# A fused RWKV and mixture-of-experts layer: the first block in halves, two of the last rows ahead of a branch, and three row accumulations between scatters

## The chip, the cores and the metric

One core of a Trainium2 chip. The metric is the device time of one execution in microseconds (us). Five engines take part, each with an instruction stream of its own: PE (TensorE, matrix products and transposes), DVE (VectorE), ACT (ScalarE), POOL (GpSimd) and SP (SyncE, which here only issues DMAs). POOL issues DMAs too: the gathers, and all DMAs that accumulate into DRAM.

## What is computed

The input x is 2048 rows of 512. Everything is float32. Cut to what matters:

```python
xn  = layernorm(x)
rvk = xn @ W_rvk.T;  r, v, k = split(rvk, 3)
att = (sigmoid(r) * wkv(time_decay, time_first, k, v)) @ W_out.T    # wkv: a recurrence over all rows
# experts: 8 routed and 4 that hand on their input, the 2 best of 12 for each row
probs = softmax(xn @ classifier_w.T); idx = top_k(probs + bias, 2); rw = 1.5 * probs[idx]
ffn = sum over the chosen e < 8: rw_e * (silu(xn @ gate_e.T) * (xn @ up_e.T)) @ down_e.T
ffn = ffn + xn * (sum of rw over the chosen e >= 8)
out = x + att + ffn
```

## The kernel before, in words

The rows stand in 16 row tiles of 128 (numbered 0 to 15), four to a block (blocks 0 to 3). The order of the instructions on every engine is the order in which the code issues them (a manual schedule); nothing reorders them later. A wait arises where a tile's producer, or the last user of its buffer, runs on another engine or is a DMA.

*Head.* SP issues the four loads of block 0 (L95), the weights of k (L102), the classifier, and the other loads. `norm(b)` (L207) takes mean and variance of four row tiles on DVE (L212, L213), then one short chain for all four: an ACT square root (L218), a reciprocal and a Newton step on DVE (L220 to L227). Then the four tiles are normalized, the even ones on DVE (L232), the odd ones on ACT (L234), and stored to DRAM as `xs` for the later gathers (L125). `turn_block(b)` (L237) transposes the block on PE, 4 chunks of 4 tiles, and ACT copies each chunk out of PSUM (L246). Blocks 1 to 3 follow in a loop, with first products (L325) and the classifier (L254, L267) between. Then comes the routing on DVE, which sorts the 4096 choices into tiles of 128 rows of one expert each.

*Middle.* The work of the scans (DVE, 16 of them: 4 blocks by 4 chunks), of the k, v, r products, and of 25 expert tiles is merged by planned times (`table`, L991 to L1025). An expert tile i is gathered from `xs` (L733, POOL), transposed by a DMA, multiplied by gate and up weights (L795, PE), activated (L803 ACT, L804 and L806 DVE), transposed again, multiplied by the down weights (L836, PE), scaled on ACT into `yo` (L840, three buffers in turn) and scattered with an add into the output (L841, POOL). The output has been set to x beforehand. Tiles are about 10.3 us apart.

The output projection of rows 0 to 7 (`attention_row`, L969) is merged in as well: PE products (L973), then DVE adds the share of the experts that hand on their input (L983). Rows 0 to 3 are accumulated into the output by POOL DMAs in two pairs (`add_row`, L967); rows 4 to 7 are put on the list `late`.

*Tail.* Behind the table, `attention(NTB - 2, [j])` does rows 8 to 11 (PE L921, DVE L934), between them the last scan's steps. Then comes a branch (L1032 to L1053): the number of tiles that are needed is loaded into every engine, and a loop over further tiles is skipped when there are no more than 25. Behind the branch `read_out` reads rows 12 to 15 of the output back (L900, SP) and adds the experts that hand on their input (L901, DVE). POOL accumulates rows 4 to 11 (L1057, L967). `attention(NTB - 1)` multiplies rows 12 to 15 (L921), adds the result on DVE (L930) and stores the row (L931); row 15 goes in two halves of 256 columns, both in one PSUM bank.

All writes into the output tensor are ordered: a scatter or an accumulation that may touch the same rows as an earlier one waits on POOL until the earlier one's data has landed. Row accumulations of different rows do not wait for each other.

PSUM has eight banks in four pools of two: `ps_mm`, `ps_gu`, `ps_o` and `ps_tr`. Row 8 to 11 take `ps_o` and `ps_mm` in turn; rows 12 and 13 take `ps_o`, 14 and 15 `ps_mm`.

Of the kernel before, what the change touches and what calls it, by code (L numbers as in the profile page):

```python
# [26 lines left out]
F32 = mybir.dt.float32  # L27
# [8 lines left out]
P = 128  # L36
T = 2048
C = 512
CC = C // P
TB = 512  # L40
NTB = T // TB
NJ = TB // P
# [9 lines left out]
TILES = 25  # L52
# [7 lines left out]
def layer(ctx: ExitStack, tc: tile.TileContext, x, w_rvk, w_out, decay, first, cls, ebias, gu, down, out):  # L60
    nc = tc.nc

    def pool(name, bufs, **kw):
        return ctx.enter_context(tc.tile_pool(name=name, bufs=bufs, **kw))
# [3 lines left out]
    place = pool("place", 1)  # L68
# [6 lines left out]
    small = pool("small", 2)  # L75
# [4 lines left out]
    ps_mm = pool("ps_mm", 2, space=bass.MemoryType.PSUM)  # L80
    ps_gu = pool("ps_gu", 2, space=bass.MemoryType.PSUM)
    ps_o = pool("ps_o", 2, space=bass.MemoryType.PSUM)
    ps_tr = pool("ps_tr", 2, space=bass.MemoryType.PSUM)
# [38 lines left out]
    def store_xn(b):  # L122
        for j in range(NJ):
            i = b * NJ + j
            nc.sync.dma_start(xs[i * P : (i + 1) * P, :], xt[i])  # L125
# [65 lines left out]
    for c in range(CC):  # L191

        s = const.tile([P, 5], F32, tag=f"state{c}", name=f"state{c}")
# [10 lines left out]
    xnT = {}  # L204
    pl = ps_o.tile([P, NT, ET], F32, tag="o", name="pl")

    def norm(b):  # L207
        js = slice(b * NJ, (b + 1) * NJ)
        for j in range(NJ):
            i = b * NJ + j  # L210
            st = small.tile([P, 6], F32, tag="st", name=f"st{i}")
            nc.vector.bn_stats(st, xt[i])  # L212
            nc.vector.bn_aggr(mv[:, i, :], st)  # L213
        var = mv[:, js, 1]
        ve = small.tile([P, NJ], F32, tag="ve", name=f"ve{b}")
        nc.vector.tensor_scalar_add(ve, var, EPS)
        sd = small.tile([P, NJ], F32, tag="sd", name=f"sd{b}")
        nc.scalar.activation(sd, var, AF.Sqrt, bias=eps_sb[:, 0:1])  # L218
        r0 = small.tile([P, NJ], F32, tag="r0", name=f"r0{b}")
        nc.vector.reciprocal(r0, sd)  # L220

        sq = small.tile([P, NJ], F32, tag="sq", name=f"sq{b}")
        nc.vector.tensor_mul(sq, r0, r0)
        nc.vector.tensor_mul(sq, sq, ve)
        nc.vector.tensor_scalar(sq, sq, -0.5, 1.5, ALU.mult, ALU.add)
        nc.vector.tensor_mul(rstd[:, js], r0, sq)
        nc.vector.scalar_tensor_tensor(shift[:, js], mv[:, js, 0], -1.0, rstd[:, js], ALU.mult, ALU.mult)  # L227
        for j in range(NJ):
            i = b * NJ + j
            t, r = xt[i], rstd[:, i : i + 1]  # L230
            if j % 2 == 0:
                nc.vector.tensor_scalar(t, t, mv[:, i, 0:1], r, ALU.subtract, ALU.mult)  # L232
            else:
                nc.scalar.activation(t, t, AF.Identity, bias=shift[:, i : i + 1], scale=r)  # L234
        store_xn(b)

    def turn_block(b):  # L237
        xnT[b] = place.tile([P, CC, TB], F32, tag=f"s{2 + b}", name=f"xnT{b}")
        for c in range(CC):
            if c % 2 == 0:  # L240
                pt = ps_tr.tile([P, TB], F32, tag="tr", name=f"pt{b}_{c}")
            else:
                pt = ps_gu.tile([P, TB], F32, tag="gu", name=f"pt{b}_{c}")
            for j in range(NJ):
                nc.tensor.transpose(pt[:, j * P : (j + 1) * P], xt[b * NJ + j][:, c * P : (c + 1) * P], ident)
            nc.scalar.copy(xnT[b][:, c, :], pt)  # L246

    lgs = {}

# [261 lines left out]
    def whole(gen):  # L511
        for _ in gen:
            pass


    manual = ExitStack()
    manual.enter_context(tc.manual_schedule())
    norm(0)
    turn_block(0)
    for b in range(NTB):  # L520
        if b + 1 < NTB:
            norm(b + 1)
        fill(1 if b else 2)
        logits(b)
        fill(1 if b else 3)
        if b + 1 < NTB:
            turn_block(b + 1)
        add_quarters(b)
# [194 lines left out]
    wplace = const.tile([P, MAX_TILES], F32, tag="wplace", name="wplace")  # L723
# [109 lines left out]
    def finish(i, weight=wplace, to=to_i):  # L833
        po = ps_o.tile([P, C], F32, tag="o", name=f"po{i}")
        for c in range(IC):
            nc.tensor.matmul(  # L836
                po, st[i]["actT"][:, c, :], st[i]["d"][:, c, :], start=(c == 0), stop=(c == IC - 1)
            )
        yo = rows.tile([P, C], F32, tag="rb", name=f"yo{i}")
        nc.scalar.activation(yo, po, AF.Identity, scale=weight[:, i : i + 1])  # L840
        nc.gpsimd.indirect_dma_start(  # L841
            out=out,
            out_offset=bass.IndirectOffsetOnAxis(ap=to[:, i : i + 1], axis=0),
            in_=yo,
            in_offset=None,
            compute_op=ALU.add,
        )
        del st[i]

    def first_half(i, n):  # L850
# [15 lines left out]
    def second_half(i, n):  # L866

        if i + 1 < n:
            unite(i + 1)
        if i + 2 < n:  # L870
            flip(i + 2)
        if i > 1:
            finish(i - 2)
        if 1 < i < n - 1:
            fetch_down(i)
        if i == n - 2:
            fetch_down(i + 1)
        if i == n - 1:
            finish(i - 1)

    xrows, orows = {}, {}
# [12 lines left out]
    def read_out(b):  # L894

        t = place.tile([P, NJ, C], F32, tag="s0", name=f"orows{b}")
        for j in range(NJ):
# [4 lines left out]
                orows[i], xrows[i], zw[:, i : i + 1], orows[i], ALU.mult, ALU.add  # L902
            )

    def attention(b, js=range(NJ)):

        for j in js:
            i = b * NJ + j
            if b < NTB - 2:
                po = ps_tr.tile([P, C], F32, tag="tr", name=f"pw{i}")  # L910
            elif j >= 2 if i in orows else j % 2 == 1:
                po = ps_mm.tile([P, C], F32, tag="mm", name=f"pw{i}")
            else:
                po = ps_o.tile([P, C], F32, tag="o", name=f"pw{i}")

            halves = 2 if i == NT - 1 else 1
            n = C // halves
            for h in range(halves):
                hs = slice(h * n, (h + 1) * n)
                for c in range(CC):  # L920
                    nc.tensor.matmul(  # L921
                        po[:, hs],
                        yT[b][:, j, c, :],
                        wout_sb[:, c, hs],
                        start=(c == 0),
                        stop=(c == CC - 1),
                    )
                    yield
                if i in orows:
                    nc.vector.tensor_add(orows[i][:, hs], orows[i][:, hs], po[:, hs])  # L930
                    nc.sync.dma_start(out[i * P : (i + 1) * P, hs], orows[i][:, hs])  # L931
            if i in orows:
                continue
            nc.vector.scalar_tensor_tensor(xrows[i], xrows[i], zw[:, i : i + 1], po, ALU.mult, ALU.add)  # L934

# [28 lines left out]
    late = []  # L964

    def add_row(n):
        nc.gpsimd.dma_start(out[n * P : (n + 1) * P, :], xrows[n], accum_op=ALU.add)  # L967
# [25 lines left out]
    def plan(at, what, *args):  # L993
        table.append((at, iter([(what, *args)]) if args else what))
# [19 lines left out]
    spread = (total - 12) / TILES  # L1014
# [4 lines left out]
    plan(7 + spread * TILES, read_xn, NTB - 1)  # L1019
    plan(4 + spread * TILES, turn_act, TILES - 1)  # L1020
    plan(7 + spread * TILES, finish, TILES - 1)
    for _, work in sorted(table, key=lambda entry: entry[0]):
        todo = next(work, None)
        if todo:
            todo[0](*todo[1:])  # L1025
    for j, stops in enumerate((1, 2, 0, 0)):
        whole(attention(NTB - 2, [j]))
        for _ in range(stops):
            next(stages[-1])


    count = nc.values_load(  # L1032
# [23 lines left out]
    read_out(NTB - 1)  # L1056
    for n in (*late, *range((NTB - 2) * NJ, (NTB - 1) * NJ)):  # L1057
        add_row(n)
    whole(attention(NTB - 1))
    manual.close()  # L1060


# [40 lines left out]
```

## Time and profile before

| what | us |
|---|---|
| median of three runs (379.75 to 383.75) | 380.06 |
| the profiled execution's own time | 379.29 |
| its span, from the first to the last instruction | 377.5 |
| busy: PE, DVE, ACT, POOL | 358.2, 308.9, 161.5, 91.4 |
| granted TensorE clock | 1.0 |

The profile is of one execution. A row of the timeline is: start, length, engine, line, operation, output<-inputs, and in brackets the idle time of the engine before it and what ended that idle time. "x16" means that so many instructions are merged into the row. A float32 product shows as two instructions of PE. A row of the chain of waits is: start, length, engine and line; "issue" is time in which nothing shows a wait. A row of DMA issues ends with the KB of one and the median us from issue to landing.

### The profile page before, as it was taken

How to read it: one execution, taken by the hardware profiler on the slowest of the kernel's cores; microseconds unless marked ns; L12 is line 12 of the kernel's file. 1: busy time of each engine (PE TensorE's matmuls, PEld its weight loads, DVE VectorE, ACT ScalarE, POOL GpSimd, SP SyncE). 2: the span in 40 equal slices, each digit the busy share in tenths (PEclk: the TensorE clock that was granted, in tenths of full speed). 3: DMA queues.
4: the chain of work that ended last, by engine and by line, in shares of the span. 5: the costliest groups of instructions: out<-in, count | busy, mean ns of one | idle time of the engine just before them, and what ended most of it. 6: DMA issues, size and time to landing. Idle time of an engine off the chain costs nothing.

```text
span 377.5 us, 3504 instructions
## 1 busy us (share of the span) xinstructions
PE 358.2 (95%) x970; PEld 164.9 (44%) x970; DVE 308.9 (82%) x450; ACT 161.5 (43%) x274; POOL 91.4 (24%) x118
## 2 busy tenths in 40 slices
PE   0899998999999999999999999999999999999995
PEld 0565444543444444444444444444444444444343
DVE  4879899989997997987987779597769786959951
ACT  1677311232653554554556453636354555423000
POOL 5000300210203233322232224133144321102450
PEclk9999999999999999999999999999999999999999
DMA  7998944643657898889898998999999999767497
GB/s 268 399 356 322 334 141 162 227 91 132 177 126 220 257 264 250 251 230 260 220 262 237 272 265 222 271 233 319 258 280 277 290 264 248 195 188 166 93 191 191
DMA packets 63029, 88.80 MB, mean 235 GB/s; under 512 B 42208, under 2 KB 42592, under 8 KB 59232
## 3 DMA queue, kind: packets, MB, share of 16 engines
q1 hardware_dynamic: 55472, 67.85, 61.5%
q0 software_dynamic: 7536, 20.71, 23.5%
q8 instruction: 8, 0.13, 0.1%
q14 instruction: 13, 0.11, 0.1%
HBM read 63.78 MB, written 19.40 MB: 220 GB/s over the span
## 4 chain that ended last, share of the span: by engine, by line
PE 73%; DVE 17%; DMA 5%; ACT 2%; issue 2%; SPq 0%; DVEq 0%
PE pg L795 22%; PE po L836 10%; PE pr L408 9%; PE py L325 9%; PE pw L973 7%; PE pz L325 6%; PE px L325 4%; PE pw L921 4%; DMA x<-in_x_dram 3%; DVE den L505 3%; DMA wrvk<-in_w_rvk_dram 2%; DVE tok L687 2%; DVE sums L490 1%; DVE obv L477 1%; DVE st L212 1%
## 5 line engine op out<-in xcount | busy, mean ns | idle before, releaser
L795 PE MATMUL pg<-gw,xgT 128*128 128x512 f32 x200 | 90.2, 593 | 1.5 <-ACT xgT L783 1.5
L841 POOL DMA_INDIRECT out_dram<-yo,to_i x25 | 45.7, 1826 | 165.0 <-ACT yo L840 114.5
L408 PE MATMUL pr<-xnT,wrvk 128*128 128x512 f32 x128 | 60.6, 593 | 0.0
L795 PEld LDWEIGHTS pg<-gw,xgT 128*128 128x128 f32 x200 | 37.8, 190 | 49.3 <-issue 45.7
L505 DVE RECIPROCAL den<-den 128x512 f32<-128x512 f32 x16 | 53.5, 3345 | 0.0
L836 PE MATMUL po<-dw,actT 128*128 128x512 f32 x100 | 46.9, 593 | 0.5 <-ACT actT L814 0.5
L803 ACT ACTIVATE th<-pg 128x256 f32<-128x256 f32 x25 | 9.6, 384 | 85.0 <-PE pg L795 85.0
L733 POOL DMA_INDIRECT xg<-xs,token_i x25 | 27.0, 1080 | 61.9 <-ACT xp L775 28.3
L408 PEld LDWEIGHTS pr<-xnT,wrvk 128*128 128x128 f32 x128 | 24.1, 190 | 29.2 <-issue 29.2
L804 DVE SCALAR_TENSOR_TENSOR th<-th,pg 128x256 f32<-128x256 f32 x25 | 10.5, 419 | 32.1 <-ACT th L803 32.0
L325 PE MATMUL px<-xnT,wrvk 128*128 128x512 f32 x64 | 32.3, 604 | 0.0
L325 PE MATMUL py<-t,wrvk 128*128 128x512 f32 x64 | 30.7, 594 | 0.0
L783 ACT COPY xgT<-xq 128x1024 uint16<-128x1024 uint16 x25 | 28.9, 1156 | 3.9 <-DMA xq<-xp 3.8
L921 PE MATMUL pw<-wout_sb,yT 128*128 128x512 f32 (+1 forms) x72 | 28.2, 548 | 2.0 <-DVE xrows L934 1.5
L973 PE MATMUL pw<-wout_sb,yT 128*128 128x512 f32 x64 | 30.1, 592 | 0.0
L836 PEld LDWEIGHTS po<-dw,actT 128*128 128x128 f32 x100 | 18.9, 190 | 24.2 <-issue 22.7
L775 ACT COPY xp<-xg 128x1024 uint16<-128x1024 uint16 x25 | 26.1, 1044 | 5.6 <-DMA xq<-xp 4.5
L840 ACT ACTIVATE yo<-po,wplace 128x512 f32<-128x512 f32 x25 | 17.2, 686 | 23.2 <-PE po L836 23.0
L490 DVE TENSOR_TENSOR_SCAN sums<-obv,state,a 128x512 f32<-128x512 f32 x16 | 20.5, 1282 | 4.1 <-ACT obv L483 4.0
L492 DVE TENSOR_TENSOR_SCAN sums<-obv,state,a 128x512 f32<-128x512 f32 x16 | 20.5, 1284 | 0.6
L921 PEld LDWEIGHTS pw<-wout_sb,yT 128*128 128x128 f32 x72 | 13.5, 190 | 17.0 <-issue 13.4
L477 DVE TENSOR_TENSOR_SCAN obv<-wdec,state,k 128x512 f32<-128x512 f32 x16 | 20.5, 1280 | 0.0
(171 smaller groups left out, 459.0 us busy)
## 6 DMA issues: line engine op xcount, KB each, us to landing
gw<-in_gu_dram SPq DMA_DIRECT2D x25, 1024.0 KB, 5.5
dw<-in_down_dram SPq DMA_DIRECT2D x25, 512.0 KB, 5.9
x<-in_x_dram SPq DMA_DIRECT2D x16, 256.0 KB, 5.3
xs<-x SPq DMA_DIRECT2D x16, 256.0 KB, 4.9
wrvk<-in_w_rvk_dram SPq DMA_DIRECT2D x3, 1024.0 KB, 7.2
xrow<-xs SPq DMA_DIRECT2D x8, 256.0 KB, 7.0
xrows<-xs SPq DMA_DIRECT2D x8, 256.0 KB, 5.2
wout_sb<-in_w_out_dram SPq DMA_DIRECT2D x1, 1024.0 KB, 10.6
```

The lines of the kernel that those rows point to most:

```text
L325: nc.tensor.matmul(ps, a[:, k, c * P : (c + 1) * P], x[:, k], start=(start and k == 0), stop=(k == 1), skip_group_check=True,)
L408: nc.tensor.matmul(ps, wrvk_sb[0][:, k, c * P : (c + 1) * P], xnT[b][:, k, :], start=(k == 0), stop=(k == CC - 1))
L477: nc.vector.tensor_tensor_scan(o2, w.to_broadcast([P, TB]), k, s[:, 0:1], ALU.add, ALU.max)
L505: nc.vector.reciprocal(den, den)
L733: nc.gpsimd.indirect_dma_start(out=xg, out_offset=None, in_=xs, in_offset=bass.IndirectOffsetOnAxis(ap=token[:, i : i + 1], axis=0),)
L775: nc.scalar.copy(xp, st[i]["xg"].bitcast(U16).rearrange("p (c h) -> p h c", h=2))
L783: nc.scalar.copy(xgT.bitcast(U16).rearrange("p c (t h) -> p c t h", h=2), st[i]["xq"].rearrange("p (h c) t -> p c t h", h=2),)
L795: nc.tensor.matmul(pg, st[i]["xgT"][:, c, :], st[i]["w"][:, c, :], start=(c == 0), stop=(c == CC - 1))
L836: nc.tensor.matmul(po, st[i]["actT"][:, c, :], st[i]["d"][:, c, :], start=(c == 0), stop=(c == IC - 1))
L841: nc.gpsimd.indirect_dma_start(out=out, out_offset=bass.IndirectOffsetOnAxis(ap=to[:, i : i + 1], axis=0), in_=yo, in_offset=None, compute ...
L921: nc.tensor.matmul(po[:, hs], yT[b][:, j, c, :], wout_sb[:, c, hs], start=(c == 0), stop=(c == CC - 1),)
L973: nc.tensor.matmul(po, yT[b][:, j, c, :], wout_sb[:, c, :], start=(c == 0), stop=(c == CC - 1))
```

## The change

Four things.

First, `norm` and `turn_block` take a part of a block. Block 0 is done in two halves of two row tiles: statistics, the short chain, normalization and the transposes of tiles 0 and 1, then those of tiles 2 and 3. ACT copies a chunk out when its second half is there. Blocks 1 to 3 are done whole as before.

Second, rows 8 to 15 get their PSUM banks by pairs: rows 8 and 9 `ps_o`, 10 and 11 `ps_tr`, 12 and 13 `ps_mm`, 14 and 15 `ps_o`. The second half of row 15 takes a bank of its own in `ps_tr`. The first product of row 8 is issued ahead of the last tile's `finish`.

Third, the products of rows 12 and 13 stand ahead of the branch. Their additions and stores stay behind it, and come when the rows read back have been prepared (`add_rows`).

Fourth, `finish` of tiles 19, 20 and 21 issues one accumulation of a late row (rows 4, 5 and 6) right behind its scatter. Row 7 and rows 8 to 11 stay behind the branch.

```diff
-    def norm(b):
-        js = slice(b * NJ, (b + 1) * NJ)
-        for j in range(NJ):
+    def norm(b, part=range(NJ)):
+        n = len(part)
+        js = slice(b * NJ + part[0], b * NJ + part[0] + n)
+        for j in part:
...
-        store_xn(b)
+        if part[-1] == NJ - 1:
+            store_xn(b)
+
+    pts = {}
 
-    def turn_block(b):
-        xnT[b] = place.tile([P, CC, TB], F32, tag=f"s{2 + b}", name=f"xnT{b}")
+    def turn_block(b, part=range(NJ)):
         for c in range(CC):
-            if c % 2 == 0:
+            if part[0] > 0:
+                pt = pts[c]
+            elif c % 2 == 0:
...
-            for j in range(NJ):
+            pts[c] = pt
+            for j in part:
                 nc.tensor.transpose(pt[:, j * P : (j + 1) * P], xt[b * NJ + j][:, c * P : (c + 1) * P], ident)
-            nc.scalar.copy(xnT[b][:, c, :], pt)
+            if part[-1] == NJ - 1:
+                if c == 0:
+                    xnT[b] = place.tile([P, CC, TB], F32, tag=f"s{2 + b}", name=f"xnT{b}")
+                nc.scalar.copy(xnT[b][:, c, :], pt)
...
-    norm(0)
-    turn_block(0)
+
+    for part in (range(0, NJ // 2), range(NJ // 2, NJ)):
+        norm(0, part)
+        turn_block(0, part)
...
             compute_op=ALU.add,
         )
+        if TILES - 7 < i < TILES - 3 and weight is wplace:
+
+            add_row(late.pop(0))
         del st[i]
...
+    whole_rows = []
+
+    def add_rows():
+
+        for i, hs, po in whole_rows:
+            nc.vector.tensor_add(orows[i][:, hs], orows[i][:, hs], po[:, hs])
+            nc.sync.dma_start(out[i * P : (i + 1) * P, hs], orows[i][:, hs])
+        whole_rows.clear()
+
     def attention(b, js=range(NJ)):
-
         for j in js:
             i = b * NJ + j
-            if b < NTB - 2:
-                po = ps_tr.tile([P, C], F32, tag="tr", name=f"pw{i}")
-            elif j >= 2 if i in orows else j % 2 == 1:
-                po = ps_mm.tile([P, C], F32, tag="mm", name=f"pw{i}")
-            else:
-                po = ps_o.tile([P, C], F32, tag="o", name=f"pw{i}")
+
+            pool_, tag = ((ps_o, "o"), (ps_tr, "tr"), (ps_mm, "mm"), (ps_o, "o"))[(i - (NTB - 2) * NJ) // 2]
+            po = pool_.tile([P, C], F32, tag=tag, name=f"pw{i}")
...
                 hs = slice(h * n, (h + 1) * n)
+                if h == 1:
+                    po = ps_tr.tile([P, C], F32, tag="tr", name=f"pw{i}_{h}")
                 for c in range(CC):
...
-                if i in orows:
-                    nc.vector.tensor_add(orows[i][:, hs], orows[i][:, hs], po[:, hs])
-                    nc.sync.dma_start(out[i * P : (i + 1) * P, hs], orows[i][:, hs])
-            if i in orows:
+                if b == NTB - 1:
+                    whole_rows.append((i, hs, po))
+                    yield
+            if b == NTB - 1:
                 continue
...
+    third = [attention(NTB - 2, [j]) for j in range(NJ)]
+    plan(6.9 + spread * TILES, third[0])
     for _, work in sorted(table, key=lambda entry: entry[0]):
         todo = next(work, None)
         if todo:
             todo[0](*todo[1:])
     for j, stops in enumerate((1, 2, 0, 0)):
-        whole(attention(NTB - 2, [j]))
+        whole(third[j])
         for _ in range(stops):
             next(stages[-1])
+    whole(attention(NTB - 1, range(0, 2)))
...
     read_out(NTB - 1)
     for n in (*late, *range((NTB - 2) * NJ, (NTB - 1) * NJ)):
         add_row(n)
-    whole(attention(NTB - 1))
+    add_rows()
+    for _ in attention(NTB - 1, range(2, NJ)):
+        add_rows()
     manual.close()
```

More of the change, by code (lines that the diff above doesn't have):

```diff
@@ L214, in norm @@
         var = mv[:, js, 1]
-        ve = small.tile([P, NJ], F32, tag="ve", name=f"ve{b}")
+        ve = small.tile([P, NJ], F32, tag="ve", name=f"ve{b}_{part[0]}")[:, :n]
         nc.vector.tensor_scalar_add(ve, var, EPS)
-        sd = small.tile([P, NJ], F32, tag="sd", name=f"sd{b}")
+        sd = small.tile([P, NJ], F32, tag="sd", name=f"sd{b}_{part[0]}")[:, :n]
         nc.scalar.activation(sd, var, AF.Sqrt, bias=eps_sb[:, 0:1])
-        r0 = small.tile([P, NJ], F32, tag="r0", name=f"r0{b}")
+        r0 = small.tile([P, NJ], F32, tag="r0", name=f"r0{b}_{part[0]}")[:, :n]
         nc.vector.reciprocal(r0, sd)
-        sq = small.tile([P, NJ], F32, tag="sq", name=f"sq{b}")
+        sq = small.tile([P, NJ], F32, tag="sq", name=f"sq{b}_{part[0]}")[:, :n]
         nc.vector.tensor_mul(sq, r0, r0)
@@ L243, in turn_block @@
                 pt = ps_gu.tile([P, TB], F32, tag="gu", name=f"pt{b}_{c}")
-            for j in range(NJ):
+            pts[c] = pt
+            for j in part:
                 nc.tensor.transpose(pt[:, j * P : (j + 1) * P], xt[b * NJ + j][:, c * P : (c + 1) * P], ident)
-            nc.scalar.copy(xnT[b][:, c, :], pt)
+            if part[-1] == NJ - 1:
+                if c == 0:
+                    xnT[b] = place.tile([P, CC, TB], F32, tag=f"s{2 + b}", name=f"xnT{b}")
+                nc.scalar.copy(xnT[b][:, c, :], pt)
     lgs = {}
```

## The prediction, made before the changed kernel was run

> **What bounds the kernel now.** I read the page's row of busy shares first, then the chain of work that ended last, then the timeline of the two ends of the span, and last the rows of the POOL queue. All times are microseconds of the span before.
>
> ```profile
> PE 358.2 (95%) x970; PEld 164.9 (44%) x970; DVE 308.9 (82%) x450; ACT 161.5 (43%) x274; POOL 91.4 (24%) x118
> ```
>
> PE is busy 95% of the span; only at the two ends does it wait. The head, from the timeline:
>
> ```profile
> 8.26 0.30 ACT L218 ACTIVATE sd<-mv,eps_sb 128x4 f32<-128x4 f32 x1 [6.01 <-DVE mv L213]
> ...
> 9.79 1.52 ACT L234 ACTIVATE x<-x,shift,rstd 128x512 f32<-128x512 f32 x2 [1.24 <-DVE shift L227]
> ...
> 10.37 3.91 PE L245 MATMUL pt<-ident,x 128*128 128x128 f32 x16 [10.37 <-DVE x L232]
> ```
>
> PE does nothing until 10.37, because block 0 is normalized as a whole and DVE waits 1.12 for the fourth load (its stats start at 7.31). The chain at the other end:
>
> ```profile
> 350.71 1.17 issue
> 351.88 0.72 DVE xrows L934
> 352.60 0.67 DVE den L497
> ...
> 354.65 3.27 DVE den L505
> 357.95 0.70 DVE yT L506
> 358.65 0.26 DVEq L1032
> 358.91 0.40 DVE xrows L934
> 359.31 0.04 issue
> 359.36 12.31 PE pw L921 x32
> 371.66 0.02 issue
> 371.69 0.43 DVE orows L930
> 372.12 0.04 issue
> 372.16 2.01 PE pw L921 x8
> 374.17 0.02 issue
> 374.20 0.42 DVE orows L930
> ```
>
> DVE ends the last scan at 358.64, PE does the last block's rows (12 to 15) from 359.36 to 374.17, then one addition and one store. POOL is not in this chain, but it gates the rows read back from the output:
>
> ```profile
> 308.02 2.50 POOL L841 DMA_INDIRECT out_dram<-yo,to_i  x1 [6.48 <-ACT yo L840]
> 318.23 1.74 POOL L841 DMA_INDIRECT out_dram<-yo,to_i  x1 [7.71 <-ACT yo L840]
> 328.62 1.55 POOL L841 DMA_INDIRECT out_dram<-yo,to_i  x1 [8.65 <-ACT yo L840]
> 339.14 1.62 POOL L841 DMA_INDIRECT out_dram<-yo,to_i  x1 [8.97 <-ACT yo L840]
> 345.08 1.55 POOL L841 DMA_INDIRECT out_dram<-yo,to_i  x1 [4.33 <-ACT yo L840]
> 350.65 1.55 POOL L841 DMA_INDIRECT out_dram<-yo,to_i  x1 [4.01 <-DVE obv L491]
> 356.23 3.65 POOL L967 DMA_DIRECT2D out_dram<-yT  x4 [4.03 <-DMA out_dram<-yo,to_i]
> ```
>
> These are the scatters of tiles 19 to 24 and the first late rows. Asked for one at a time, the DMA issues of the six scatters land 8.9, 7.3, 8.3, 5.1, 4.7 and 4.8 after their start. The last three starts lie 5.94, 5.57 and 5.58 apart: each starts 0.84 to 0.87 after the one before has landed. All accumulate into one tensor, so each waits for the last. The reads of the output (L900) start at 355.62, 0.17 after the last scatter landed (355.45). Up to 339.14 the queue waits for ACT; from there it is a chain without slack.
>
> **The change part by part.**
>
> Head. Tiles 0 and 1 no longer wait for 2 and 3. Added: seven small DVE operations of 0.16 to 0.18 and one ACT square root of 0.30. Small chain and one normalization of the first half fill DVE from 5.1 to 7.2, so the statistics of tiles 2 and 3 (at 5.29 and 7.31 before) move to 7.2 and 8.0; their chain ends 0.7 later, but has one DVE normalization less ahead of block 1, which starts 0.3 later than 10.66. ACT's normalization of tile 3 ends at about 11.2 (before 11.31). By then PE has done 8 of 16 transposes; the other 8, at 0.21 each (3.91 for 16, with a wait), end at 12.95 where the 16 ended at 14.1. The products that follow at 14.11 have their weights (the 1 MB load issued at 2.61 lands 7.2 later). PE works almost without a break from 14.11 to 22, and the next square root waits for ACT's copies behind it, so I take 1.1 off everything behind. Bounds: a gain of 1.2, and a loss of 0.3 if DVE's delay were what carries.
>
> Row 8's first product ahead of tile 24's last. It fills the 0.52 that PE waited at 342.12 for ACT's copy: 0.45 off PE. Its bank is free in time.
>
> Rows 12 and 13 ahead of the branch. PE's last pass of row 11 starts at 357.27, so PE is free at 357.70, 1.66 before 359.36; less the 0.45, at 357.25. Row 12's first three products need chunks 0 to 2 only, and its fourth comes at 359.8, past 358.64. Their banks are those of the products, long free. So 1.66 off. The other side is the branch, before covered by PE's wait (at most 1.4, from 357.84 to 359.26): now PE meets it after row 13, with nothing to cover it. DVE went through the same branch in at most 0.21 (idle ahead of its 360.17). Bounds +0.2 and +1.4; I take 0.5, nearer to DVE's row since that is a branch crossed by an engine with work behind it.
>
> A bank for the second half of row 15. The wait of 0.51 at 372.16 for DVE's addition goes: −0.5. Sum on PE's path: −0.45 − 1.66 − 0.5 + 0.5 = −2.1. The four additions of rows 12 to 15 on DVE stay, in the same order, and the same five stores on SP.
>
> Three accumulations between scatters. In the built program's POOL queue the row adds stand one each behind the scatters of tiles 19, 20 and 21, ahead of 20, 21 and 22, and each waits for the scatter ahead of it, as the scatter behind waits for the add. So this isn't filling idle POOL time: it makes a chain of nine. Behind it wait: ACT's output of tiles 23 and 24 (three buffers: they need scatters 20 and 21 landed), and through the last scatter SP's four reads, the five row adds left, and DVE's four L901. No gather is behind it (the last is ahead of scatter 19).
>
> What does one add cost? The rows: four mid-run adds, in two pairs, land 7.6 to 8.3 after issue with weight loads in flight; the first of the eight at the end lands at 7.6. No add is seen alone. Lower bound: the shortest scatter, 4.7, less 0.7 as an add holds POOL 0.9 and a scatter some 1.6: 4.0. I take 7.6 for row 4 (DMA is at 90% there, like the pairs) and 5.0 for rows 5 and 6, nearer to the quiet scatters, since the DMA share is low around 337 to 341 and 349 to 353. With 0.85 after each landing:
>
> - scatter 19 at 308.02, lands 316.9; row 4 at 317.8, lands 325.4
> - scatter 20 at 326.25 (before 318.23), 7.3, lands 333.55; row 5 at 334.4, lands 339.4
> - scatter 21 at 340.25 (before 328.62), 5.1, lands 345.35; row 6 at 346.2, lands 351.2
> - scatter 22 at 352.05 (before 339.14), 23 at 357.6, 24 at 363.15, lands 367.95; reads at 368.1 (before 355.62)
>
> Tile 24's output on ACT waits from 344.1 to 345.4; the exponential behind it is due at 347.45, so that costs nothing unless scatter 21 is 1.4 later still.
>
> End from the reads on. Before, the last L901 ended 9.58 after the reads began. Then come five additions on DVE, three of 0.69 and two of 0.42, overlapping: 2.6. The last store lands 1.7 after issue when alone, the whole rows 4.7 to 6.8; four stores now crowd into 2.6, so 4.5. Together 16.7 (bounds 14.8 and 19). The adds agree: queue 0 took 56.8% of the last 22, that is 1.56 per row; five rows from 0.6 after the reads, 7.6 for the first and 4 x 1.56: 14.4.
>
> Sum: 368.1 + 16.7 − 1.1 = 383.7 of span, plus the 1.8 around it (379.29 − 377.5): **385.5**. PE's path alone would give 379.29 − 1.1 − 2.1 = 376.1 and lies hidden. The profiled execution's 379.29 is 0.8 under the median, 380.06; I leave the sum on the profiled one.
>
> The Trainium skill ("DMA: Bandwidth & Descriptors", section "Anatomy of one DMA") speaks against the price: a transfer from GpSimd costs about 2.0 plus its bytes at 436 GB/s, so 2.6 for 256 KB. The first load of x, from SP, did land in 2.6, but no accumulate here came below 4.7. By its 2.6 for the three adds the reads would start 9.8 earlier, at 358.3, and the whole come out at the 376.1 of PE's path.
>
> **The rivals.**
>
> Hidden after all (ends on the other side). If adds and scatters were short, PE's path would set the end: 376.1. The point that decides: reads no later than 376.1 − 1.8 + 1.1 − 16.7 = 358.7, 3.1 later than before; with the fixed legs (8.9, then 4.7, 4.7, 4.8, and 0.85 between) rows 4 to 6 and scatters 20 and 21 would have to land in 4.1 each on average. For it: 56.8% of 22 over eight adds is only 1.56 of DMA time each. Against: no accumulate landed in under 4.7.
>
> Partly absorbed. All legs at their low ends (adds 4.0, scatter 20 at 6.1, 21 at 5.1) put the reads at 361.3, and with the low tail of 14.8 the time is 376.8; with the tail of 16.7, 378.7. Between this and my sum lies 377 to 382, hardly slower than before.
>
> Everything loaded. Adds at 8.3, scatters 20 and 21 at 8.3 and 7.3: scatter 21 lands at 352.5, tile 24's output and the exponential behind it are some 5 late and DVE's last scan with them, and the reads start at about 379. Time up to 379 + 16.7 − 1.1 + 1.8 = 396. Against: the two windows without DMA load.
>
> **How the numbers follow.** Chances: late reads as summed (382 to 391) 0.62, partly absorbed (377 to 382) 0.20, hidden (376.1) 0.08, everything loaded (over 391) 0.10. The range leaves out hidden and loaded: 378 to 391. Within 1% of 380.06 is 376.3 to 383.9, about what a measurement of this kernel can tell from no change. Faster by more: half of hidden, 0.04. Within: the other half, partly absorbed, and the low edge of my case, 0.04 + 0.20 + 0.06 = 0.30. Slower: 0.66.
>
> **What would show it.** Right: scatter 22 starts past 345, the reads past 362, DVE waits for the reads of the output while PE is long done with row 15, and PE's first product starts near 13. Wrong: adds alone landing in under 5 with the reads before 360; then PE is in the chain to the end, and the branch on PE is the only thing left to pay. If tile 24's output on ACT starts past 347, the exponential behind it is late too.

## The result and the profile after

| what | before | after |
|---|---|---|
| median, 20 runs each (us) | 379.71 (377.79 to 383.75) | 386.81 (383.56 to 391.35) |
| the profiled execution's own time, its span | 379.29, 377.5 | 385.03, 383.2 |
| reads of the output start (in the span) | 355.62 | 367.08 |
| PE ends its last product | 374.17 | 371.54 |

The changed kernel is slower: 1.0176 times the time before, with an interval of 1.0154 to 1.0199. Comparisons leave out executions more than 1.5% above the fastest of the same kernel; where a kernel's own executions lie that far apart, they are told one by one.

PE is no longer what the end waits for. The row of busy shares of the kernel after:

```profile
PE 359.7 (94%) x970; PEld 165.5 (43%) x970; DVE 309.5 (81%) x457; ACT 162.0 (42%) x275; POOL 93.0 (24%) x118
```

Its busy time is that of before plus 1.5, while the span is 5.7 longer. PE's last group in the timeline:

```profile
344.36 27.18 PE L942 MATMUL pw<-wout_sb,yT 128*128 128x512 f32 x70
```

54 full passes at 0.43 and 16 half ones at 0.25 make 27.2: there is no gap in it, not for the branch and not for a bank. PE is done at 371.54 and the span goes on for 11.7. The chain of waits of the kernel after, its last part:

```profile
362.08 4.80 DMA out_dram<-yo,to_i
...
367.96 5.61 DMA orows<-out_dram
...
373.67 0.76 DVE orows L915
...
376.28 1.26 DVE orows L924 x3
```

Before, this chain went through the last scan on DVE and row 12 to 15 on PE. Now it goes from the last scatter through the rows read back (367.96 to 373.58) to DVE. The POOL rows of the timeline show why these reads are late:

```profile
308.36 2.50 POOL L852 DMA_INDIRECT out_dram<-yo,to_i  x1 [4.59 <-ACT yo L851]
317.19 0.96 POOL L988 DMA_DIRECT2D out_dram<-yT  x1 [6.33 <-DMA out_dram<-yo,to_i]
324.82 1.61 POOL L852 DMA_INDIRECT out_dram<-yo,to_i  x1 [6.67 <-ACT actT L838]
330.46 0.92 POOL L988 DMA_DIRECT2D out_dram<-yT  x1 [4.03 <-DVE v L384]
338.55 1.89 POOL L852 DMA_INDIRECT out_dram<-yo,to_i  x1 [7.17 <-DMA out_dram<-yT]
344.37 0.91 POOL L988 DMA_DIRECT2D out_dram<-yT  x1 [3.92 <-DVE den L514]
350.34 2.12 POOL L852 DMA_INDIRECT out_dram<-yo,to_i  x1 [5.07 <-DMA out_dram<-yT]
356.52 1.56 POOL L852 DMA_INDIRECT out_dram<-yo,to_i  x1 [4.06 <-issue]
362.08 1.55 POOL L852 DMA_INDIRECT out_dram<-yo,to_i  x1 [4.00 <-DMA out_dram<-yo,to_i]
```

L852 is a scatter, L988 a row accumulation. Nine DMAs stand in one line, and each of the eight behind the first starts when the one before it has landed. Issue to landing, asked for one at a time, is 8.3, 6.8, 5.0, 7.3, 5.2, 5.0, 5.4, 4.7 and 4.8. The names in the brackets mislead in three places (ACT actT, DVE v, DVE den): a wait for several semaphores is put down to one of them, but each start lies 0.5 to 1.0 behind the landing of the DMA ahead.

The head of the kernel after, from the timeline of PE:

```profile
7.20 2.05 PE L251 MATMUL pt<-ident,x 128*128 128x128 f32 x8 [7.20 <-DVE x L233]
10.70 2.14 PE L251 MATMUL pt<-ident,x 128*128 128x128 f32 x8 [1.44 <-DVE x L233]
12.63 3.62 PE L334 MATMUL px<-xnT,wrvk 128*128 128x512 f32 x4
16.19 1.16 PE L263 MATMUL lg<-xnT,cls_sb 128*32 128x512 f32 x8
```

PE starts 3.2 earlier than before (10.37) and the first products 1.5 earlier (before 14.11). But four of them take 3.62, before 1.88, and the classifier's products behind them start 0.27 later than before (15.92).

### The profile page after: what moved, and what is told of

Same layout as the page of the kernel before. It is cut to its first block, busy times and chain, and to the rows that moved or that the text cites. A ratio compares the mean times of both kernels' runs of the same rounds, so it can differ in the third digit from the quotient of the medians.

```text
span 383.2 us, 3515 instructions
## 1 busy us (share of the span) xinstructions
PE 359.7 (94%) x970; PEld 165.5 (43%) x970; DVE 309.5 (81%) x457; ACT 162.0 (42%) x275; POOL 93.0 (24%) x118
## 5 line engine op out<-in xcount | busy, mean ns | idle before, releaser
L852 POOL DMA_INDIRECT out_dram<-yo,to_i x25 | 45.4, 1817 | 157.0 <-ACT yo L851 77.3
L744 POOL DMA_INDIRECT xg<-xs,token_i x25 | 28.7, 1149 | 61.8 <-ACT xp L786 28.2
L815 DVE SCALAR_TENSOR_TENSOR th<-th,pg 128x256 f32<-128x256 f32 x25 | 10.5, 418 | 32.1 <-ACT th L814 32.0
L334 PE MATMUL px<-xnT,wrvk 128*128 128x512 f32 x64 | 34.0, 633 | 0.0
```

Of the source, the lines that this page charges most:

```text
L334: nc.tensor.matmul(ps, a[:, k, c * P : (c + 1) * P], x[:, k], start=(start and k == 0), stop=(k == 1), skip_group_check=True,)
L744: nc.gpsimd.indirect_dma_start(out=xg, out_offset=None, in_=xs, in_offset=bass.IndirectOffsetOnAxis(ap=token[:, i : i + 1], axis=0),)
L852: nc.gpsimd.indirect_dma_start(out=out, out_offset=bass.IndirectOffsetOnAxis(ap=to[:, i : i + 1], axis=0), in_=yo, in_offset=None, compute ...
```

## The experiments

Each edit is made to the kernel after, unless it says "to the kernel before".

**Are the accumulations the cause?** Two kernels: the change without them, and they alone.

*e1_no_adds*

```diff
-        if TILES - 7 < i < TILES - 3 and weight is wplace:
-            add_row(late.pop(0))
```

> The changed kernel with rows 4 to 6 accumulated behind the branch as before; all else of the change stays. Theory (the chain of nine waits on POOL sets the end, the rest of the change is a gain): the reads of the output start at about 356, scatter 22 at about 339, PE's last product ends near 371.5 as in the changed kernel's trace (before: 374.2), time 377.0 to 378.0 against 379.7 before. Rival A (the accumulations are not the cause; something else of the change slows the end): 384 or more. Rival B (eight row accumulations behind the branch, the last of which landed at 374.8 before, become the bound as soon as PE is earlier): 379 to 380, no gain.

Measured: 378.85, ratio 0.9985 (0.9961 to 1.0009), the kernel before on the same chip 379.96 in the median. The 1.8% are gone, so the three accumulations are the whole loss. But the kernel isn't faster than before to a degree that this can tell, though the sum for PE's path promised 3.2, and the 377.0 to 378.0 that I expected were missed. PE behind the branch in e1_no_adds, from the timeline:

```profile
368.26 7.12 PE L939 MATMUL pw<-wout_sb,yT 128*128 128x512 f32 x24 [0.15 <-PEq L1059]
```

And its last row accumulation, from the DMA issues (KB of one and us to landing at the end of a row):

```profile
out_dram<-xrows POOLq DMA_DIRECT2D x1, 256.0 KB, 10.5
```

PE waits 0.15 at the branch. The last row accumulation, issued at 367.91, lands at 378.4, 3 after PE's last product. (This profiled execution, 382.83, is a long one for this kernel: PE waited 2.39 for a transposed tile at 311.63, and the eight passes behind that pause took 5.40, not 3.60. Only what is read relative to its own reads is used.)

*e2_adds_only*, to the kernel before

```diff
+        if TILES - 7 < i < TILES - 3 and weight is wplace:
+            add_row(late.pop(0))
```

> The kernel before with nothing but the three accumulations behind the scatters of tiles 19 to 21. Theory: the reads start 10.5 to 12 later than 355.6 and the time is 385 to 388, as for the whole change, since what PE gains elsewhere is hidden behind them. Rival (the slowdown needs the new order of the tail, the adds alone are absorbed): 381 or less.

Measured: 387.43, ratio 1.0224 (1.0176 to 1.0272); reads at 366.13. The accumulations alone cost all of the loss. Whether they cost more than the whole change, so that the rest of it wins something even when the reads are late, the times don't show: the two intervals overlap. But from the reads to the end of the span it is 18.6 here and 16.2 in the kernel after, and the timeline of PE in e2_adds_only shows where:

```profile
377.64 3.78 PE L924 MATMUL pw<-wout_sb,yT 128*128 128x256 f32 x8 [6.39 <-DVE orows L933]
```

Both halves of row 15 share a bank here, so the second waits 6.39 for DVE to add the first, and DVE waits for the late reads. After this pause the eight half passes take 3.78, not 1.99. With a bank of its own for the second half (the kernel after) PE has neither.

**Is it their number, or that they alternate with the scatters?**

*e5_one_add* and *e6_two_adds*

```diff
-        if TILES - 7 < i < TILES - 3 and weight is wplace:
+        if TILES - 7 < i < TILES - 5 and weight is wplace:    # e5_one_add; e6_two_adds: TILES - 4
```

> The changed kernel with one accumulation only (row 4, behind the scatter of tile 19); rows 5 and 6 go back behind the branch. Theory (a chain of waits that first uses up the idle time of POOL's queue): scatter 20 starts near 325 and scatter 21 near 331, but scatter 22 waits for ACT's output as before, so the reads start at about 356 and the time is that of the kernel without any of the three, 378.5 to 379.5. Rival (each accumulation costs its share, the three together 8): 381 to 382.

> The changed kernel with two accumulations (rows 4 and 5, behind the scatters of tiles 19 and 20); row 6 goes back behind the branch. Theory, with the steps measured in the changed kernel's trace: scatter 21 at 338.5, 22 at 344.6, the reads at 360.6, 16.3 later the end: 378.5 to 380.5. Rival (each costs its share): 384.

Measured: one accumulation 379.97, ratio 0.9978 (0.9939 to 1.0016), its executions spread from 376.4 to 386.0 (before, on the same chip, 379.75 in the median); two 383.5, 1.0109 (1.0068 to 1.0149). With none, one, two and three the ratios are 0.9985, 0.9978, 1.0109 and 1.0176: not a share for each. The first costs nothing that can be told, since before the change the queue waited for ACT between scatters 19 and 22. The starts there were 10.21, 10.39 and 10.52 apart, the landings 8.9, 7.3 and 8.3, and POOL needs 0.85 more: 0.5, 2.2 and 1.4 to spare, 4.1 in all. For three accumulations: 6.8, 7.3 and 5.0 of landing and 0.6 each for the additional gap make 20.9; less the 4.1; less 6.0, as scatters 19 to 21 land 6.0 sooner in sum in the kernel after; that is 10.8. From scatter 19 to scatter 22 it was 10.9 more (41.98 against 31.12), and the reads came 11.5 later.

e6_two_adds read at 360.90, as expected (360.6), but ended 19.0 after its reads, not 16.3, and its 383.5 is near the rival's 384, not the 378.5 to 380.5 that I expected. So the end behind the reads isn't a constant. In the profiled executions it grows with the number of accumulations left behind the branch: 16.2 and 17.4 with five (after, e4), 18.1 to 19.0 with six (e6, e9, e10), 19.7 and 19.9 with seven (e11, e5), and 21.5 with eight (e1_no_adds, 359.45 to 381.0; e12 too). An accumulation moved ahead thus also takes a little off the end: of the 11.5 that the reads were later in the kernel after, 5.7 reached its span.

*e4_adds_bunched*

```diff
-        if TILES - 7 < i < TILES - 3 and weight is wplace:
-            add_row(late.pop(0))
+        if i == TILES - 5 and weight is wplace:
+            while late:
+                add_row(late.pop(0))
```

> The changed kernel, but its three accumulations issued together behind the scatter of tile 20, so that they wait for one scatter and not for each other's neighbours. Theory (the cost is three waits in a row, not the data): the three land within some 9 of the first's issue, scatter 21 starts near 336, scatter 22 near 342, the reads near 358.5, time 377.0 to 378.5. Rival (three accumulates cost what they cost wherever they stand in the queue): the reads at 366 or later and 385 or more.

Measured: 379.58, ratio 1.0001 (0.9971 to 1.0031). The same three accumulations, at one place, cost 1.7% less than one at a time. So it isn't their DMA time alone; it is that each waits for a scatter and a scatter waits for each. By the code rows don't wait for each other, so three at once are one member of the chain. The gain of 0.5 to 0.8% that I expected besides did not come. The profiled execution is the longest of the thirteen (386.46). Its POOL rows, from scatter 19 on:

```profile
314.92 2.51 POOL L852 DMA_INDIRECT out_dram<-yo,to_i  x1 [6.48 <-ACT yo L851]
...
333.06 2.76 POOL L988 DMA_DIRECT2D out_dram<-yT  x3 [6.20 <-DVE act L817]
344.47 2.54 POOL L852 DMA_INDIRECT out_dram<-yo,to_i  x1 [8.66 <-ACT r L421]
```

The three land in 4.0 to 9.3, and scatter 21 starts 11.4 after the first of them; in the kernel after, the three members take 7.6, 8.1 and 6.0 to the next scatter, 21.7 together. So in the trace too they are one member. The reads come at 367.29 even so, as late as in the kernel after, because scatter 19 starts 6.6 later here. It starts anywhere from 307.6 to 314.9 in the profiled executions that have no accumulation right ahead of it, so the reads are best counted from it: 43.5 to 48.7 with none between the scatters (before, e1, e3, e7, e8, e12), 47.4 with one (e5), 50.9 with two (e6), 52.4 with three at one place (e4), 58.7 and 58.5 with three one at a time (after, e2). This is one execution of each kernel; why scatter 19 varies is open.

*e9_pair_early*: rows 4 and 5 at once behind the last gather, ahead of scatter 19; none behind scatters 19 to 21.

```diff
-        if TILES - 7 < i < TILES - 3 and weight is wplace:
-            add_row(late.pop(0))
...
+        if i == TILES - 4:
+            while late:
+                add_row(late.pop(0))
```

> The changed kernel with rows 4 and 5 accumulated together one tile earlier, behind the scatter of tile 18 and the last gather; row 6 goes back behind the branch. It has as many accumulations ahead of the branch as the kernel with two of them. Theory (what counts is whether the queue has caught up by scatter 22): the pair starts near 306 and has landed by 316, scatters 19 to 21 start near 317, 324 and 331, scatter 22 at 339 as without any, the reads at 356, and the six row accumulations behind the branch in place of eight end 3 earlier: 376.5 to 378.5. Rival (two accumulations cost what two cost): 382 to 384.

Measured: 380.43 over all twelve executions, ratio 0.9979 (0.9938 to 1.0021), above the 376.5 to 378.5 that I expected. As many accumulations as in e6_two_adds, 1.3% less time. But the executions fall into groups: three at 375.7 to 377.1, six at 379.7 to 380.8, three at 382.2 to 385.9. In the POOL rows of the profiled one (380.71) the pair makes scatter 19 late:

```profile
307.77 1.90 POOL L988 DMA_DIRECT2D out_dram<-yT  x2 [4.60 <-DVE den L514]
318.56 1.72 POOL L852 DMA_INDIRECT out_dram<-yo,to_i  x1 [8.89 <-ACT yo L851]
329.75 1.56 POOL L852 DMA_INDIRECT out_dram<-yo,to_i  x1 [9.46 <-ACT a L491]
338.22 2.09 POOL L852 DMA_INDIRECT out_dram<-yo,to_i  x1 [6.91 <-DMA out_dram<-yo,to_i]
```

The pair lands by 317.7, scatter 19 starts at 318.56 and lands 10.3 after issue (before 8.9), and the reads are at 360.75. Counted from scatter 19 that is 42.2, less than the 47.6 before, so the queue makes up a part.

*e11_row4_early_busy*: row 4 alone at that place, and a PE kept busy in the head (below).

> The changed kernel with row 4 alone accumulated behind the scatter of tile 18 and the last gather, rows 5 and 6 back behind the branch, and the 52 transposes of the identity in the head. Theory: one accumulation of some 8 is absorbed by the idle time of POOL's queue ahead of scatter 22 even where scatters take 8 to 9, so that the reads start at 355 to 357; seven row accumulations behind them, and 0.9 off in the head: 377 to 378.5. Rival (even one makes the queue late in most executions): 379.5 or more.

Measured: 382.14 over all twelve, before 379.94; eleven lie at 381.1 to 383.9 and one at 376.12. That is the rival's 379.5 or more, though the ratio, which rests on the five shortest, is 1.0002 (0.9958 to 1.0045). In the profiled one row 4 took 10.6 to land, and the queue was late again (scatter 19 at 317.88, reads at 359.60). So one accumulation ahead of scatter 19 can put the queue behind. That it is worse there than behind scatter 19 (e5_one_add) isn't shown: the two intervals overlap, and the profiled e5_one_add reads at 360.95. Nor is it clear why two rows at that place (e9_pair_early) took less time than one.

**Why did the head not give 1.1?**

*e3_halves_only*, to the kernel before: `norm` and `turn_block` of the change, nothing else.

```diff
-    norm(0)
-    turn_block(0)
+    for part in (range(0, NJ // 2), range(NJ // 2, NJ)):
+        norm(0, part)
+        turn_block(0, part)
```

> The kernel before with nothing but the first block in halves. Theory from the trace after (PE starts 3.2 earlier, but its first products run at 0.86 a pass in place of 0.43, and the routing begins at 38.2 in place of 37.8): 379.7 to 380.2, no gain. Rival (my prediction: 1.1 less, the late routing was chance): 378.6.

Measured: 380.0, ratio 1.0001 (0.9978 to 1.0024). The halves bring nothing. The four products take 3.32 from 12.69, and the routing on DVE starts at 37.85 (before 37.84).

*e7_halves_busy*, to the kernel before: the same, with transposes ahead of each half whose result nobody reads.

```diff
+    idle = ps_mm.tile([P, TB], F32, tag="mm", name="idle")
+    def keep_busy(n):
+        for m in range(n):
+            nc.tensor.transpose(idle[:, m % NJ * P : (m % NJ + 1) * P], ident, ident)
+    keep_busy(32)
     for part in (range(0, NJ // 2), range(NJ // 2, NJ)):
         norm(0, part)
         turn_block(0, part)
+        if part[0] == 0:
+            keep_busy(20)
```

> The kernel before with the first block in halves, and 52 transposes of the identity that nothing reads, 32 ahead of the first half and 20 between the halves, so that PE has no pause up to the first products. Theory (halves gained nothing because PE, which paused for 1.4 between the halves, ran its first products at 0.86 a pass): the passes take 0.43 and the routing starts 1 to 2 earlier, 377.7 to 378.8. Rival (the gain is lost to ACT or DVE, whatever PE does): 379.5 to 380.5.

Measured: 379.07, ratio 0.9986 (0.9964 to 1.0007). The head of e7_halves_busy in the timeline of PE:

```profile
1.98 6.34 PE L532 MATMUL idle<-ident 128*128 128x128 f32 x32 [1.98 <-POOL ident masks.py:199]
...
12.31 1.99 PE L334 MATMUL px<-xnT,wrvk 128*128 128x512 f32 x4
...
17.73 1.12 PE L334 MATMUL px<-xnT,wrvk 128*128 128x512 f32 x2 [0.53 <-ACT v L352]
```

Four products take 1.99 now, and the routing starts at 36.92, 0.9 earlier than before. The other profiled executions agree. With the halves alone the four products take 2.64 to 3.62 and the routing starts at 37.34 to 38.19 (eight kernels, 37.86 in the mean), no earlier than with the block done whole (37.84 before, 37.46 in e2_adds_only). With the busy PE they take 1.98 or 1.99 and it starts at 36.78 to 37.56 (four kernels, 37.12 in the mean). So the slow passes were what ate the head's gain up to the routing. Of the 1.1 some 0.7 in the mean then reach it (ACT is the next late one, 0.53 at 17.73), but whether they reach the end the times can't tell: 379.07 is above the 377.7 to 378.8 that I expected.

**Where did the tail's gain go?**

*e8_no_rows*: e1_no_adds without the eight row accumulations behind the branch, so the output lacks them.

```diff
-    for n in (*late, *range((NTB - 2) * NJ, (NTB - 1) * NJ)):
-        add_row(n)
```

> The changed kernel without the three accumulations and without those of rows 4 to 11 behind the branch; the output lacks what they add. Theory (without the chain of waits, what PE gains at the end is given back because the last stores land among the last row accumulations): PE's last product ends where it does with them, the last store lands in some 2 in place of 4.0, 376 to 377.3. Rival (the accumulations land beside the stores at no cost): the same as with them, 378.9.

Measured: 377.54, ratio 0.9942 (0.9919 to 0.9964), just above the 376 to 377.3 that I expected. PE ends at 371.43, 2.74 earlier than before, and the span of the profiled execution is 2.4 shorter. The last store of e8_no_rows, from its DMA issues:

```profile
out_dram<-orows SPq DMA_DIRECT2D x1, 128.0 KB, 1.7
```

The same of e1_no_adds:

```profile
out_dram<-orows SPq DMA_DIRECT2D x1, 128.0 KB, 4.0
```

So the gain on PE's path is there, and this ratio is clearly below 1. With the row accumulations (e1_no_adds) 0.4% of it, some 1.6, is given back: the last store takes 4.0 among them, not 1.7. In the kernel before it also took 1.7, issued when the last accumulation had all but landed (374.64, 374.75). The size of the 1.6 is uncertain, as the two intervals just touch; the two kernels were run on different chips, each against the kernel before on its own.

**Can a version beat both?**

*e12_no_adds_busy* (e1_no_adds with the busy head) and *e10_pair_early_busy* (e9_pair_early with it).

> The changed kernel without the three accumulations, and with the 52 transposes in the head. Theory (eight row accumulations behind the branch set the end, counted from the reads, which start 0.9 earlier with the head): 377.5 to 378.5. Rival (the head's gain does not reach the end): 378.9, as without the transposes.

> The same with the 52 transposes of the identity in the head. Theory: 0.5 to 1 less than the kernel without them, 375.7 to 377.8, below both the kernel before and the changed one. Rival (the head's gain is lost in the middle): the same time as without them.

Measured: e12_no_adds_busy 0.9971 (0.9947 to 0.9996), the only version with the whole output whose interval lies below 1, by a hair; over all twelve its median is 379.69, before 379.94, so this doesn't show it faster. e10_pair_early_busy 0.9995 (0.9954 to 1.0035), two executions at 375.4, one at 378.6 and nine at 380.4 to 382.2: the 375.7 to 377.8 that I expected were missed. In the profiled execution of e12_no_adds_busy PE is done at 372.16, 2.0 earlier than before; the last accumulation lands at 375.4, the stores of half rows take 4.8 in the median, and the span is 377.9, 0.4 more than before. If the ratio holds, 1.1 of PE's gain reaches the time (0.29% of 380).

## Why the prediction was right, step by step

The time came out 1.3 above the forecast by medians and 0.5 below it by the profiled execution (385.03). The mechanism is that of the forecast. Inside the sum the head, single prices and the parts of the end were wrong, and that they cancelled was luck.

- *The chain of nine waits: right.* e1_no_adds and e2_adds_only show that the three accumulations are the whole loss, e4_adds_bunched that it is the alternation. The reads were put at 368.1 − 1.1 = 367.0 and came at 367.08.
- *The prices of its members: right in sum, not one by one.* Row 4 was put at 7.6 (measured 6.8), scatter 20 at 7.3 (5.0), row 5 at 5.0 (7.3), row 6 at 5.0 (5.0), scatter 21 at 5.1 (5.2); the nine landings at 53.1 (52.5). I gave the loaded price to scatter 20 and the quiet one to row 5; it was the other way round. From a landing to the next issue I took 0.85: a scatter needed 0.78 to 0.97, a row only 0.53 to 0.64.
- *The head, −1.1: wrong.* The step that fails is "I take 1.1 off everything behind". The products started 1.5 earlier, at 12.63, but took 3.62 in place of 1.88, which the sum left out; the routing started no earlier (e3_halves_only, e7_halves_busy). Scatter 19 started 1.5 later than the sum has it (308.36 against 306.9), but as it varies by 7 between executions that says nothing on the head. The shorter landings (0.6) and gaps (0.8) made up for it, so the reads were on time by luck.
- *The branch, +0.5 on PE: too much.* Nothing in the kernel after, 0.15 in e1_no_adds.
- *Row 8's product, rows 12 and 13, row 15's bank: right in sum.* Without the head's 1.1 and the branch's 0.5 the three terms make 2.61, and PE's end came 2.63 earlier. The bank is worth more than the 0.5 when the reads are late (e2_adds_only).
- *From the reads to the end, 16.7: right in sum.* 16.2 measured: 7.9 to the first of the five additions (9.58 forecast), 2.54 for these (2.6), 5.7 for the last stores (4.5).
- *Rival "Hidden": its point of decision was right, its time wrong.* Reads at 358.7 or earlier let PE's path set the end, and without accumulations between scatters the reads came at 356.40 (e12_no_adds_busy). But such a kernel takes 378.85 and not 376.1, since the head's 1.1 isn't there and the transfers at the end give back some 1.6. Had the rival come true, its price would have failed.
- *Rival "Partly absorbed".* It needed landings of 4.0 for each accumulation; they took 5.0 to 7.3, and 4.7 was the shortest of any that stood alone (e6_two_adds). What is absorbed is the first one, by the 4.1 that the queue had to spare, and the range 377 to 382 is where one accumulation falls, or three at one place.
- *Rival "Everything loaded".* Tile 24's output on ACT starts at 344.56, ahead of the 347 that was its sign, so it did not come. Longer landings than it assumed do occur, behind accumulations ahead of scatter 19: up to 10.3 for a scatter (e9_pair_early), 10.6 for row 4 itself (e11_row4_early_busy).

From the fit in the Trainium skill ("DMA: Bandwidth & Descriptors", section "Anatomy of one DMA") follows an estimate of 2.6 for a transfer of 256 KB that GpSimd issues; the three accumulations between scatters took 6.8, 7.3 and 5.0, and the measurement decides.

## What to carry to other kernels

DMAs that accumulate into one tensor and wait for one another are a chain: price a new member by its landing plus the gap to the next issue, set against it the time that the queue had to spare up to the next thing that reads the tensor, and put members that need no order among themselves at one place. A gain at the end of one engine's path is worth only what the transfers that land there leave of it. An engine that starts earlier, with a pause behind its first work, hasn't gained until its rate is up.

## What the runs showed of the hardware that I had not expected

- PE's rate after a start. In the kernel after, PE pauses 1.44 between the halves, and float32 passes start 0.86 apart and last 1.06 each until about 16.2, then 0.43 and 0.59. That is 5.5 after the restart at 10.70, and 9 after the first start at 7.20. Before, without the long pause, PE was at 0.43 from 14.11, 3.7 after its start. But the pause isn't why the one is longer than the other: in e2_adds_only, with the block done whole, passes still start 0.85 apart at 13.04 and 13.89, and full rate comes some 5.3 after the start at 9.21; in e7_halves_busy, busy without a pause from 1.98, the transposes are 0.21 apart up to 7.2 and 0.11 from 7.5. What the pause does is that the work ahead of it doesn't count: in the eight kernels with halves and no busy PE full rate comes some 3.5 to 5.6 after the restart, which is 7 to 9 after the first start.
- The slow rate comes back after pauses. After 6.39 eight half passes took 3.78 instead of 1.99 (e2_adds_only); after 3.91 (e4_adds_bunched, 271.80) and 2.39 (e1_no_adds, 311.63) eight passes took 6.74 and 5.40 instead of 3.60. After 1.87 (e3_halves_only, 270.07) they took 3.70. So mid-run a pause of 1.87 did no harm here and one of 2.39 did.
- The profile's granted clock is 0.50 in the slow stretches of mid-run (e2 377.6 to 381.4, e4 271.8 to 277, e1 313 to 315). For the one in the head of the kernel after, 12.6 to 16.2, it is 1.00, as for 0 to 5 where PE hasn't begun. So in the head it doesn't show the slow rate; the duration of a pass does.
- The Trainium skill ("TensorE: Matmul & The Clock Gate", section "Part 1: The HAM clock gate (the "warmup" mystery)") says that TensorE runs at half rate until it has been busy for a window of about 3.4 us, which runs freely, and goes back after an idle one. The 3.7, 5.3 and 5.5 from the start of work without a pause agree: by an estimate from the page's figure a whole window of work ends 3.4 to 6.8 after the work starts. The pauses of 6.39 and 3.91 agree too; the one of 2.39 is shorter than a window, and there the measurement decides.
- The mean granted clock of an execution, 1.00 before and 0.989 after, is no sign of slower work here: in the kernel after it is 1.00 in the head and from 340 to 371.5, while PE works, and 0.50 from 375 to the end, when PE has been done since 371.54.
- A row accumulation of 256 KB landed in 4.7 to 10.6 alone between scatters (after, e2, e5, e6, e11), in 3.9 to 9.3 in a group of two or three (e4, e9, e10), and in 10.5 to 10.8 as the last of eight. Scatter 19 behind an early pair took 10.3 (e9) and 9.8 (e10).
